# A second layer's loop recast: half images in program order, edge blocks by masked weights, stores on two queues

## The chip, the cores and the metric

The kernel runs on one core of a Trainium2 chip. The metric is the device time of one execution in microseconds (us), the median of the runs. Five engines work side by side: TensorE (PE, with its weight loads as PEld), VectorE (DVE), ScalarE (ACT), GpSimd (POOL) and SyncE (SP). SP and ACT each issue DMAs from their own instruction queue.

## The reference, cut to what matters

Two layers run on a batch of 32 images of 8 channels and 256 x 256 pixels, in f32. Layer 0 (a gated cellular automaton) takes most of the time and is left alone by the change. Layer 1 is a normalised, quantised 3 x 3 convolution with a residual:

```python
x = x + L0(_gn(x), ...)                      # layer 0; its result is called y below
v = _gn(x)                                   # group norm over channel pairs
sx = 127 / max(abs(v)); sw = 127 / max(abs(weight))
qx = clip(round(v * sx), -127, 127)
qw = clip(round(weight * sw), -127, 127)
out = x + (conv3x3(qx, qw) / (sx * sw) + bias)
```

The maximum is taken over all 32 images, so layer 1 can't quantise anything before layer 0 has ended.

## The kernel before, in words

Layer 0 writes its result y to DRAM (`y_s`), image by image, with zero rows above and below, and keeps the mean, the reciprocal deviation and the largest deviation of each image. The second layer (the block `with ExitStack() as two`, from L936) then does one image after the other.

An image is held as 19 blocks (NB) of 128 partitions: 16 rows of 8 channels, the blocks 14 rows apart (STEP), so that a block yields 14 finished rows and its two outer rows are borders; the last block yields 4. One partition of one block is a row of 256 pixels. A 3 x 3 convolution of a block is then three matmuls, one for each horizontal shift, with 128 x 128 weights that join rows and channels.

For image b the loop does this:

- a load (L947) brings all 19 blocks to `yb` (2432 KB, four buffers); the first three are issued by SP, all later ones by ACT, three images ahead;
- DVE subtracts the mean and scales (L978) in three instructions: the first block, the 17 in the middle and the last block, since the first and last use scales (`qs[:, 1]`, `qs[:, 2]`) that are zero for rows outside the image; DVE rounds by adding and subtracting a large constant (L982) and clips into a bf16 tile `qt` whose rows have 258 columns, of which 256 are written (L984);
- PE takes two blocks at a time (10 groups) into one of 4 PSUM buffers, three matmuls each (L991), and ACT brings each group to the f32 tile `ob` with scale and bias (L992); `ob` has two buffers of a whole image;
- DVE adds y to `ob` (L995), and SP stores it in 19 DMAs, one for a block (L998: 18 of 112 KB and one of 32 KB).

The order of instructions on each engine isn't that of the program text: a scheduler places them by its own estimates. In the list that it made, DVE does two additions, then the quantising of two images, and so on in pairs.

Each DMA of SP and ACT signals its landing on one of eight semaphores (called lanes here), which the framework hands out in turn over both queues. A DMA waits on its issuing engine until the DMA that had its lane last, eight places earlier, has landed. Tiles that are used again also wait: `ob` for the stores of two images before.

Of the kernel before, what the change touches and what calls it, by code (L numbers as in the profile page):

```python
# [31 lines left out]
F32 = mybir.dt.float32  # L32
BF16 = mybir.dt.bfloat16
F32R = mybir.dt.float32r
AF = mybir.ActivationFunctionType
ALU = mybir.AluOpType
AX = mybir.AxisListType
DRAM = bass.MemoryType.DRAM
PSUM = bass.MemoryType.PSUM

P = 128
C = 8
# [4 lines left out]
MAX_Q = 127.0  # L47
ROUND = 1.5 * 2.0**23

NB = 19  # L50
STEP = 14
PW = W + 2
# [61 lines left out]
def kernel(  # L114
# [15 lines left out]
    nc = tc.nc  # L130
    B = x.shape[0]
    V, S, G, T = nc.vector, nc.scalar, nc.gpsimd, nc.tensor

    def dram_ap(t, offset, dims):
        return bass.AP(t.tensor, t.offset + offset, dims)
# [5 lines left out]
    masks = cp.tile([P, 4], F32, name="masks")  # L141
# [11 lines left out]
    qw = cp.tile([P, 3, P], BF16, name="qw")  # L153
# [6 lines left out]
    mean_y = cp.tile([P, B], F32, name="mean_y")  # L160
    rstd_y = cp.tile([P, B], F32, name="rstd_y")
# [11 lines left out]
    with tc.tile_pool(name="prep", bufs=1) as pp, tc.tile_pool(name="prep2", bufs=2) as pp2:  # L173
# [24 lines left out]
        for t, n, w in (  # L198
# [3 lines left out]
            k = 64 if w == W else 43  # L202
# [63 lines left out]
    with ExitStack() as one:  # L266
# [4 lines left out]
        pool = lambda name, bufs, **kw: one.enter_context(  # L271
            tc.tile_pool(name=name, bufs=bufs, reuse_waits="tile", **kw)
        )
# [122 lines left out]
        def lattice(g):  # L396
# [81 lines left out]
            if g == 0:  # L478
                units[0], dmas = load(0)
                for d in dmas:  # L480
                    nc.sync.dma_start(*d)
                for ts in tiles:
                    begin(units[0], ts)
            for c in range(C):
                u = g * C + c
                ds = units[u]
                for step in range(STEPS):
                    if step == 7 and u + 1 < NG * C:
                        units[u + 1], dmas = load(u + 1)
                        later.extend(dmas)  # L490
# [375 lines left out]
        def chain(*gens):  # L866
            for gen in gens:
                yield from gen
# [15 lines left out]
        def both(a, t_a, b, t_b):  # L884

            done_a = done_b = 0.0
            while a or b:
                if b is None or a and done_a * t_b <= done_b * t_a:
                    w = next(a, None)
                    if w is None:  # L890
                        a = None
                        continue
                    done_a += w
                else:
                    w = next(b, None)
                    if w is None:
                        b = None
                        continue
                    done_b += w
                yield w  # L900

        def prep(g, groups=((0, 1), (2, 3))):
            return normalise([(b, gs) for gs in groups for b in range(g * GB, g * GB + GB)])

        def images(f, g):
            for b in range(g * GB, g * GB + GB):
                yield from f(b)
# [3 lines left out]
        def after(g, gen):  # L911

            while issued[0] < stored[g]:
                yield 4.0
            yield from gen
# [3 lines left out]
        for g in range(NG):  # L919
            fill, t = images(nca, g), T_NCA  # L920
            if g:
                fill, t = both(fill, t, after(g - 1, images(gate, g - 1)), T_GATE), t + T_GATE
            if g + 1 < NG:
                fill, t = both(fill, t, prep(g + 1), T_PREP), t + T_PREP
            if g == 0:
                fill, t = chain(prep(0, ((1,), (2, 3))), fill), t + 30.0
# [9 lines left out]
    with ExitStack() as two:  # L936


        pool = lambda name, bufs, **kw: two.enter_context(
            tc.tile_pool(name=name, bufs=bufs, reuse_waits="tile", **kw)  # L940
        )
        tp, qp, op, sp, yp = pool("tp", 1), pool("qp", 2), pool("op", 2), pool("sp", 1), pool("yp", 4)
        ps = pool("ps", 4, space=PSUM)

        def load(b):
            y = yp.tile([P, NB, W], F32, name="yb", tag="yb")
            (nc.sync if b < 3 else nc.scalar).dma_start(  # L947
                y, dram_ap(y_s[b], 0, [[W, P], [STEP * C * W, NB], [1, W]])
            )
            return y  # L950

        ys = {b: load(b) for b in range(3)}

        gmax = sp.tile([P, 1], F32, name="gmax")
        V.tensor_reduce(gmax, dev_y, AX.X, ALU.max)
        gall = sp.tile([P, 1], F32, name="gall")
        G.partition_all_reduce(gall, gmax, P, bass.bass_isa.ReduceOp.max)
        sx = sp.tile([P, 1], F32, name="sx")
        V.reciprocal(sx, gall)
        V.tensor_scalar(sx, sx, MAX_Q, None, ALU.mult)  # L960
        inv = sp.tile([P, 1], F32, name="inv")
        V.tensor_tensor(inv, sx, sw, ALU.mult)
        V.reciprocal(inv, inv)
        qs = sp.tile([P, 3, B], F32, name="qs")
        V.tensor_scalar(qs[:, 0, :], rstd_y, sx, None, ALU.mult)
        V.tensor_scalar(qs[:, 1, :], qs[:, 0, :], masks[:, 2:3], None, ALU.mult)
        V.tensor_scalar(qs[:, 2, :], qs[:, 0, :], masks[:, 3:4], None, ALU.mult)
        qt = [qp.tile([P, NB, PW], BF16, name=f"qt{i}", tag=f"qt{i}", bufs=1) for i in range(2)]
        for t in qt:
            V.memset(t[:, :, 0], 0.0)  # L970
            V.memset(t[:, :, PW - 1], 0.0)

        for b in range(B):
            y = ys.pop(b)

            t = tp.tile([P, NB, W], F32, name="tq", tag="tq")
            for k0, k1, i in ((0, 1, 1), (1, NB - 1, 0), (NB - 1, NB, 2)):
                V.tensor_scalar(  # L978
                    t[:, k0:k1, :], y[:, k0:k1, :], mean_y[:, b : b + 1], qs[:, i, b : b + 1],
                    ALU.subtract, ALU.mult,  # L980
                )
            V.tensor_scalar(t, t, ROUND, ROUND, ALU.add, ALU.subtract)  # L982
            q = qt[b % 2]
            V.tensor_scalar(q[:, :, 1 : 1 + W], t, MAX_Q, -MAX_Q, ALU.min, ALU.max)  # L984
            o = op.tile([P, NB, W], F32, name="ob", tag="ob")
            for p in range(10):
                k0, n = 2 * p, (2 if p < 9 else 1)
                pt = ps.tile([P, 512], F32, name="pt2", tag="pt2")
                pt = pt[:, : n * W].rearrange("p (k w) -> p k w", w=W)
                for dx in range(3):  # L990
                    T.matmul(pt, qw[:, dx, :], q[:, k0 : k0 + n, dx : dx + W], start=(dx == 0), stop=(dx == 2))  # L991
                S.activation(o[:, k0 : k0 + n, :], pt, AF.Identity, bias=bv[:, 3:4], scale=inv)  # L992
            if b + 3 < B:
                ys[b + 3] = load(b + 3)
            V.tensor_tensor(o, o, y, ALU.add)  # L995
            for k in range(NB):
                rows = STEP if k < NB - 1 else 4
                nc.sync.dma_start(  # L998
                    dram_ap(out, b * C * H * W + STEP * k * W, [[W, rows], [H * W, C], [1, W]]),
                    o[C : C + rows * C, k, :],  # L1000
                )


# [43 lines left out]
```

## Time and profile before

| what | value |
|---|---|
| median of three runs | 14070.34 us (14065.71 to 14084.15) |
| the profiled execution | 14065.15 us, span 14063.3 us |
| second layer, from its first load's issue | 13284.2 us to the end, some 779 us |
| second layer, from its first scaling (L978) | 13300.35 us to the end, 763 us |
| engine time in 13284 to 14064 us | DVE 523.9, PE 272.6, ACT 219.7, POOL 0.9 us |
| mean DMA rate there | 189 GB/s |

An engine's idle time is put down to what ended it; "q" after an engine's name means its instruction queue, as SP's when it issues a DMA. A chain of waits is followed back from the last instruction: each piece is the work, or the issue or flight of a DMA, that the next one waited for.

### The profile page before, as it was taken

The numbers are of one execution on the slowest core, as the hardware profiler recorded it, in microseconds if no ns is written. First come the engines' busy times: TensorE is split into PE (matmuls) and PEld (weight loads), VectorE is DVE, ScalarE is ACT, GpSimd is POOL, SyncE is SP. The second block draws the span as 40 slices with busy tenths as digits, with TensorE's granted clock in tenths as the row PEclk, the third lists the DMA queues.
The fourth block names the chain that finished last, engine by engine and source line by source line (L and its number), as shares of the span: only waits on it lengthen the run. The fifth ranks groups of instructions, "written<-read, shape, count | busy, mean of one in ns | idle before, by whom it ended". The sixth has DMA issues, their size and how long they took to land. (4 is left out here: it accounts for less than half of the span.)

```text
span 14063.3 us, 229517 instructions
## 1 busy us (share of the span) xinstructions
PE 13110.3 (93%) x81744; PEld 6304.1 (45%) x81744; DVE 8273.9 (59%) x16310; ACT 4036.2 (29%) x6274; POOL 2483.6 (18%) x4270
## 2 busy tenths in 40 slices
PE   5999999999999999999999999999999999999733
PEld 2444444444444444444444444444444444443211
DVE  5555555556556655566556656566556555555566
ACT  2233223222323232332223232332233222221132
POOL 1001111112111111111111211121112111112300
PEclk8999999999999999999999999999999999999966
DMA  6444444444444444444444444444444433333465
GB/s 150 96 103 97 91 108 106 114 94 104 106 110 97 102 105 105 103 103 102 108 100 105 109 99 100 110 107 97 101 108 112 98 81 87 87 84 79 124 188 179
DMA packets 2287208, 1496.74 MB, mean 106 GB/s; under 512 B 1096576, under 2 KB 2257152, under 8 KB 2285952
## 3 DMA queue, kind: packets, MB, share of 16 engines
q1 hardware_dynamic: 2210224, 1409.05, 42.8%
q10 hardware_dynamic: 75856, 73.02, 1.6%
q8 instruction: 664, 10.88, 0.3%
q14 instruction: 464, 3.80, 0.1%
HBM read 866.48 MB, written 478.69 MB: 96 GB/s over the span
## 5 line engine op out<-in xcount | busy, mean ns | idle before, releaser
L511 PE MATMUL pt<-m_a,lw 128*64 128x390 f32 x17280 | 5843.1, 496 | 157.1 <-DMA m_a<-m_a 109.3
L511 PE MATMUL pt<-m_b,lw 128*64 128x384 f32 x17280 | 5808.3, 491 | 18.8 <-DVE m_b L430 17.9
L601 ACT ACTIVATE h<-ph,bp_sb 128x512 f32<-128x512 f32 x4096 | 2585.1, 685 | 5283.9 <-PE ph L591 5209.8
L511 PEld LDWEIGHTS pt<-m_a,lw 128*64 128x64 f32 x17280 | 2298.1, 137 | 1795.2 <-issue 1633.3
L511 PEld LDWEIGHTS pt<-m_b,lw 128*64 128x64 f32 x17280 | 2304.3, 137 | 1649.5 <-issue 1550.6
L519 DVE SCALAR_TENSOR_TENSOR gt<-pt,d_a 128x384 f32<-128x384 f32 x2880 | 1581.5, 549 | 2005.2 <-PE pt L511 2005.0
L519 DVE SCALAR_TENSOR_TENSOR gt<-pt,d_b 128x390 f32<-128x390 f32 x2880 | 1607.0, 558 | 1939.0 <-PE pt L511 1936.4
L591 PE MATMUL ph<-im,wp_hi 48*128 48x512 f32 x12288 | 2621.1, 412 | 89.6 <-DMA im<-xp_s 59.0
L591 PE MATMUL ph<-im,wp_lo 48*128 48x512 f32 x12288 | 2509.9, 395 | 0.0
L528 POOL TENSOR_TENSOR m_b<-m_b,junk 128x12 f32<-128x12 f32 x2688 | 843.6, 314 | 8554.4 <-DVE m_b L524 8156.8
L591 PEld LDWEIGHTS ph<-im,wp_hi 48*128 48x128 f32 x12288 | 1239.8, 186 | 931.5 <-DVE m_b L524 185.8
L524 DVE SCALAR_TENSOR_TENSOR m_b<-gt 128x390 f32<-128x390 f32 x2688 | 1553.5, 578 | 47.0 <-DVE gt L519 0.5
L524 DVE SCALAR_TENSOR_TENSOR m_a<-gt 128x384 f32<-128x384 f32 x2688 | 1541.4, 573 | 18.1
L591 PEld LDWEIGHTS ph<-im,wp_lo 48*128 48x128 f32 x12288 | 1239.6, 186 | 229.9
L608 PE MATMUL acc<-h,wu_z 128*32 128x512 f32 x8320 | 1159.6, 600 | 6.5 <-ACT nca L626 5.5
L799 PE MATMUL pa<-cmb,gw 128*64 128x512 f32 (+1 forms) x3840 | 864.3, 580 | 14.8 <-POOL cmb L723 14.8
L799 PE MATMUL pa<-nb,gw 128*64 128x512 f32 (+1 forms) x3840 | 846.4, 573 | 0.0
L799 PE MATMUL pa<-xnb,gw 128*64 128x512 f32 (+1 forms) x3840 | 841.4, 571 | 0.0
L812 ACT ACTIVATE r<-pa,bv 128x512 f32<-128x512 f32 x320 | 213.2, 666 | 1758.0 <-PE pa L799 1757.9
L991 PE MATMUL pt<-qt,qw 128*128 128x512 bf16 (+1 forms) x960 | 270.9, 453 | 476.2 <-ACT ob L992 424.4
L729 DVE TENSOR_SCALAR xnb<-xb,sc 128x256 f32<-128x256 f32 x608 | 311.9, 528 | 578.0 <-DMA xb<-in_x_dram 569.8
L723 POOL COPY cmb<-cq 128x256 f32<-128x256 f32 x608 | 412.9, 706 | 915.5 <-DMA cq<-cm_s 775.6
(132 smaller groups left out, 7001.6 us busy)
## 6 DMA issues: line engine op xcount, KB each, us to landing
im<-xp_s SPq DMA_DIRECT2D x1152, 193.5 KB
im<-xp_s SPq DMA_DIRECT2D x1216, 96.8 KB
d_a<-xq_s SPq DMA_DIRECT2D x2048, 36.0 KB
nb<-nc_s SPq DMA_DIRECT2D x288, 256.0 KB
cq<-cm_s SPq DMA_DIRECT2D x288, 256.0 KB
yb<-y_s ACTq DMA_DIRECT2D x29, 2432.0 KB
xb<-in_x_dram SPq DMA_DIRECT2D x544, 128.0 KB
xp_s<-hi SPq DMA_DIRECT2D x256, 258.0 KB
```

What stands on the lines that cost most here:

```text
L511: T.matmul(pt[half], lw[:, c, k, half], beside if part == 2 else own, start=part < 2, stop=part > 0,)
L519: V.scalar_tensor_tensor(gt, pt, FLOOR, d[:, ts, :], ALU.max, ALU.add)
L524: V.scalar_tensor_tensor(to, gt, 1.0, gt, ALU.subtract, ALU.mult)
L528: G.tensor_tensor(edge, edge, junk.unsqueeze(1).to_broadcast([P, 6, 2]), ALU.mult)
L591: T.matmul(ph[:, :n].rearrange("p (h w) -> p h w", w=W), w[64 * i : 64 * i + 48, dx, :], rhs[:, :, dx : dx + W], start=(dx == 0 and w is w ...
L601: S.activation(h[:, :n], ph[:, :n], AF.Relu, bias=bp_sb)
L608: T.matmul(acc[32 * g : 32 * g + 32, :cols], wu_z[:, 24 - 8 * i : 56 - 8 * i], h, start=first, stop=last,)
L723: G.tensor_copy(cmb[:, k, 1 : 1 + W].rearrange("p (j q) -> p j q", q=4), cq[:, k, :].rearrange("p (q j) -> p j q", q=4),)
L729: V.tensor_scalar(xnb[:, k, 1 : 1 + W], xb[:, k, :], sc[:, i : i + 1], sc[:, 1:2], ALU.subtract, ALU.mult,)
L799: T.matmul(three[half], gw[:, s * 3 + dx, half], t[:, :n, dx : dx + W], start=(i == 0), stop=(i == 8),)
L812: S.activation(r1[:, : n * W], pa[:, : n * W], AF.Relu, bias=bv[:, 0:1])
L991: T.matmul(pt, qw[:, dx, :], q[:, k0 : k0 + n, dx : dx + W], start=(dx == 0), stop=(dx == 2))
```

## The change

Only the second layer changes. It does the following.

1. The whole block is put under `tc.manual_schedule()`: each engine's instructions keep the order of the program text.
2. An image is worked in two halves, of 10 and 9 blocks. `tq` and `ob` are half images (two and four buffers), `qt` has a tile for each half and parity, and PSUM has 8 buffers.
3. Scaling uses one scale for all blocks. Rounding and the lower clip share an instruction (add, then max), and the upper clip shares one with the subtraction that ends the rounding (min, then subtract). The latter writes `qt` in pieces of 10, 8 and 1 blocks.
4. Rows outside the image are made zero by weights: `qwm` holds two copies of the weights with the rows outside set to zero. The first block of an image and the last have matmuls of their own with them, so an image takes 33 matmuls, of which 9 have 256 columns.
5. The loop is a pipeline by one image. In round b, DVE quantises image b and then adds y to image b-1; SP stores the first 13 blocks of b-1; PE and ACT convolve b; then ACT stores the last 6 blocks of b-1 and loads image b+3 (the buffer that b-1 had).
6. SP issues the first four loads. The zero borders of `qt` are set by POOL instead of DVE.

```diff
+        two.enter_context(tc.manual_schedule())
-        tp, qp, op, sp, yp = pool("tp", 1), pool("qp", 2), pool("op", 2), pool("sp", 1), pool("yp", 4)
-        ps = pool("ps", 4, space=PSUM)
+        tp, qp, op, sp, yp = pool("tp", 2), pool("qp", 1), pool("op", 4), pool("sp", 1), pool("yp", 4)
+        ps = pool("ps", 8, space=PSUM)
...
-            (nc.sync if b < 3 else nc.scalar).dma_start(
+            (nc.sync if b < 4 else nc.scalar).dma_start(
...
+        qwm = sp.tile([P, 2, 3, P], BF16, name="qwm")
+        for i in range(2):
+            V.tensor_scalar(qwm[:, i], qw, masks[:, 2 + i : 3 + i], None, ALU.mult)
...
-            for k0, k1, i in ((0, 1, 1), (1, NB - 1, 0), (NB - 1, NB, 2)):
...
-            V.tensor_scalar(t, t, ROUND, ROUND, ALU.add, ALU.subtract)
-            V.tensor_scalar(q[:, :, 1 : 1 + W], t, MAX_Q, -MAX_Q, ALU.min, ALU.max)
+        HALVES = ((0, 10), (10, NB))
+        def scaled(b, y, h):
...
+            V.tensor_scalar(
+                t, y[:, h0:h1, :], mean_y[:, b : b + 1], qs[:, b : b + 1], ALU.subtract, ALU.mult
+            )
+            V.tensor_scalar(t, t, ROUND, ROUND - MAX_Q, ALU.add, ALU.max)
...
+        def quantised(b, t, h):
+            for k0, k1 in ((0, 10),) if h == 0 else ((0, 8), (8, 9)):
                 V.tensor_scalar(
+                    qt[b % 2][h][:, k0:k1, 1 : 1 + W], t[:, k0:k1, :], ROUND + MAX_Q, ROUND,
+                    ALU.min, ALU.subtract,
                 )
...
+                runs = [(0, n, qw)]
+                if h0 + k0 == 0:
+                    runs = [(0, 1, qwm[:, 0]), (1, n, qw)]
+                elif h0 + k0 == NB - 1:
+                    runs = [(0, 1, qwm[:, 1])]
...
+        last = None
+        for b in range(B + 1):
+            if b < B:
+                y = ys[b]
+                ts = [scaled(b, y, h) for h in range(2)]
+                for h in range(2):
+                    quantised(b, ts[h], h)
+            if last:
+                i, os_ = last
+                yi = ys.pop(i)
+                for h, (h0, h1) in enumerate(HALVES):
+                    o = os_[h][:, : h1 - h0, :]
+                    V.tensor_tensor(o, o, yi[:, h0:h1, :], ALU.add)
+                store(nc.sync, i, os_[0], 0, range(0, 10))
+                store(nc.sync, i, os_[1], 1, range(10, 13))
+            done = last
+            if b < B:
+                last = b, [convolved(b, h) for h in range(2)]
+            if done:
+                i, os_ = done
+                store(nc.scalar, i, os_[1], 1, range(13, NB))
+                if i + 4 < B:
+                    ys[i + 4] = load(i + 4)
```

More of the change, by code (lines that the diff above doesn't have):

```diff
@@ L950, in load @@
             return y
-        ys = {b: load(b) for b in range(3)}
+        ys = {b: load(b) for b in range(4)}
         gmax = sp.tile([P, 1], F32, name="gmax")
@@ L963 @@
         V.reciprocal(inv, inv)
[L964 to L971, printed above, removed]
@@ L973 @@
-        for b in range(B):
-            y = ys.pop(b)
-            t = tp.tile([P, NB, W], F32, name="tq", tag="tq")
-            for k0, k1, i in ((0, 1, 1), (1, NB - 1, 0), (NB - 1, NB, 2)):
+        qs = sp.tile([P, B], F32, name="qs")
+        V.tensor_scalar(qs, rstd_y, sx, None, ALU.mult)
+        qwm = sp.tile([P, 2, 3, P], BF16, name="qwm")
+        for i in range(2):
+            V.tensor_scalar(qwm[:, i], qw, masks[:, 2 + i : 3 + i], None, ALU.mult)
+        qt = [[qp.tile([P, n, PW], BF16, name=f"qt{i}{j}") for j, n in enumerate((10, 9))] for i in range(2)]
@@ new lines @@
+        for t in (*qt[0], *qt[1]):
+            G.memset(t[:, :, 0], 0.0)
+            G.memset(t[:, :, PW - 1], 0.0)
+        HALVES = ((0, 10), (10, NB))
+        def scaled(b, y, h):
+            h0, h1 = HALVES[h]
+            t = tp.tile([P, 10, W], F32, name="tq", tag="tq")[:, : h1 - h0, :]
+            V.tensor_scalar(
+                t, y[:, h0:h1, :], mean_y[:, b : b + 1], qs[:, b : b + 1], ALU.subtract, ALU.mult
+            )
+            V.tensor_scalar(t, t, ROUND, ROUND - MAX_Q, ALU.add, ALU.max)
+            return t
@@ L978 @@
+        def quantised(b, t, h):
+            for k0, k1 in ((0, 10),) if h == 0 else ((0, 8), (8, 9)):
                 V.tensor_scalar(
-                    t[:, k0:k1, :], y[:, k0:k1, :], mean_y[:, b : b + 1], qs[:, i, b : b + 1],
-                    ALU.subtract, ALU.mult,
-                )
[L982 to L985, printed above, removed]
@@ L986, with convolved @@
-            for p in range(10):
-                k0, n = 2 * p, (2 if p < 9 else 1)
+                    qt[b % 2][h][:, k0:k1, 1 : 1 + W], t[:, k0:k1, :], ROUND + MAX_Q, ROUND,
+                    ALU.min, ALU.subtract,
+                )
+        def convolved(b, h):
+            h0, h1 = HALVES[h]
+            o = op.tile([P, 10, W], F32, name="ob", tag="ob")
+            for k0 in range(0, h1 - h0, 2):
+                n = min(2, h1 - h0 - k0)
                 pt = ps.tile([P, 512], F32, name="pt2", tag="pt2")
@@ L989 @@
                 pt = pt[:, : n * W].rearrange("p (k w) -> p k w", w=W)
-                for dx in range(3):
-                    T.matmul(pt, qw[:, dx, :], q[:, k0 : k0 + n, dx : dx + W], start=(dx == 0), stop=(dx == 2))
+                runs = [(0, n, qw)]
[3 more added lines that the diff above has]
+                    runs = [(0, 1, qwm[:, 1])]
+                for i, j, w in runs:
+                    for dx in range(3):
+                        T.matmul(
+                            pt[:, i:j, :], w[:, dx, :],
+                            qt[b % 2][h][:, k0 + i : k0 + j, dx : dx + W],
+                            start=(dx == 0), stop=(dx == 2),
+                        )
@@ L992, with store @@
                 S.activation(o[:, k0 : k0 + n, :], pt, AF.Identity, bias=bv[:, 3:4], scale=inv)
[L993 to L996, printed above, removed]
+            return o
+        def store(queue, b, o, h, ks):
+            for k in ks:
                 rows = STEP if k < NB - 1 else 4
-                nc.sync.dma_start(
+                queue.dma_start(
                     dram_ap(out, b * C * H * W + STEP * k * W, [[W, rows], [H * W, C], [1, W]]),
-                    o[C : C + rows * C, k, :],
+                    o[C : C + rows * C, k - HALVES[h][0], :],
```

## The prediction

> **What bounds the kernel now.** The change touches only the second layer, so I read that stretch first, cut into stretches of 95 to 96 us: the busy time by stretch.
>
> ```profile
> 13615.00:13711.00 96.00, 33.67 (x123) 13.72 (x122) 64.96 (x24) 27.82 (x42) 0.00 (x0) 0.64 0.62 192
> 13711.00:13806.00 95.00, 32.52 (x119) 13.24 (x118) 64.95 (x24) 26.93 (x40) 0.00 (x0) 0.64 0.62 193
> ```
>
> Columns: us, PE, PEld, DVE, ACT, POOL, clock, DMA share, GB/s. The 24 DVE instructions are four images' worth (six each), so an image takes some 23.85 us; DVE works 16.2 to 16.5 of them, PE about 8.3, ACT 6.9, and the DMA engines 62%. No unit is full, so it is a chain of waits. Next view: who waited for whom, first on the engines, then on SP's queue.
>
> ```profile
> ACT ob L992 <- DMA out_dram<-ob: 478.4, 30, 26.3
> PE pt L991 <- ACT ob L992: 424.4, 30, 25.5
> ```
>
> ```profile
> SPq L998 <- DMA yb<-y_s: 124.5, 26, 12.0
> SPq L998 <- DVE ob L995: 49.8, 12, 4.5
> ```
>
> ACT can't bring an image to `ob` before the image two earlier is stored; PE stands behind ACT. The stores are late on SP, and in 26 places a store waited not for data but for a load: it needed that load's lane. The chain of waits, in order of time, shows one such place:
>
> ```profile
> 13605.80 2.12 DMA out_dram<-ob
> 13608.17 0.79 ACT ob L992
> 13609.00 3.88 PE pt L991 x9
> 13612.91 1.64 ACT ob L992 x3
> 13614.54 10.63 DMA yb<-y_s
> 13625.18 0.82 SPq L998
> 13626.11 0.81 SPq L998
> 13626.97 0.82 SPq L998
> ```
>
> A load issued by ACT at 13614.54 lands 10.63 us later, and only then does SP go on storing. SP's bill for an image: 19 stores at 0.895 us from start to start (two in 1.79 us in the chain, 13625.18 to 13626.97), 17.0 us, plus 3.9 us (124.5/32) behind loads, plus some 3 us, most of it waiting for DVE's additions: 23.85. DVE's rows, by form:
>
> ```profile
> L984 DVE TENSOR_SCALAR qt<-tq 128x4864 bf16<-128x4864 f32 x32 | 167.1, 5221 | 123.0 <-PE pt L991 121.4
> L995 DVE TENSOR_TENSOR ob<-ob,yb 128x4864 f32<-128x4864 f32 x32 | 167.1, 5221 | 95.9 <-ACT ob L992 76.9 <-DMA out_dram<-ob 19.0
> L982 DVE TENSOR_SCALAR tq<-tq 128x4864 f32<-128x4864 f32 x32 | 86.2, 2694 | 1.1
> L978 DVE TENSOR_SCALAR tq<-yb,mean_y,qs 128x4352 f32<-128x4352 f32 x32 | 81.3, 2540 | 0.0
> L978 DVE TENSOR_SCALAR tq<-yb,mean_y,qs 128x256 f32<-128x256 f32 x64 | 26.1, 408 | 0.7
> ```
>
> L984 and L982 have one tensor input and equal counts; one takes twice as long.
>
> **What the Trainium skill says.** "VectorE: DVE Perf Modes", What auto-detection actually checks: a one-source operation in SBUF takes the double rate if the outermost counts of source and destination are both even or equal. The trace agrees: L984 writes 19 gapped rows from a tile that can be read as one run and costs 1.07 ns an element; L376 casts 1024 elements into an even number of gapped rows in 0.689 us, 0.67 ns an element with its fixed part. "DMA: Bandwidth & Descriptors", Issuing engines are not separate DMA queues: a second issuing engine saves only issue time, the 16 DMA engines are shared. Here issue time is what SP is short of, and at 62% there is room. Same page, Anatomy of one DMA: a DMA's wait for a semaphore is on the issuing sequencer, so everything behind it stands too; SP's 124.5 us show it, and ACT will now have such waits.
>
> **The change part by part.**
>
> *DVE.* From L982 and L978: a double-rate element is 0.5205 ns, with a fixed part of 0.162 us (constants) or 0.275 us (per-partition scalars); L995 with the 512-element L762 (0.69 us) gives 1.041 ns and 0.157 us at the single rate. Scaling, 2560 and 2304 elements: 1.61+1.47. Rounding with lower clip: 1.50+1.36. Upper clip, 10, 8 and 1 blocks, all even or contiguous: 1.50+1.23+0.30 = 3.03 for 5.22. Additions: 2.82+2.56. Sum 14.35, with 11 gaps of 0.04 us 14.8 us an image (before 16.5). If the clip stays single-rate: 17.2.
>
> *PE.* 24 matmuls of 512 and 9 of 256 columns, at the before's means (0.473 and 0.272) 13.8 busy, though pipelined: 30 matmuls ran in 7.9 to 8.5 us from first to last. Eight PSUM buffers let it run a round ahead. Hidden; it would have to pass 17 us to count.
>
> *SP.* 13 stores for 19: 11.6 us. *ACT.* ten activations (9 x 0.778 + 0.567 = 7.6 us), 6 stores and one load. A store issued by ACT isn't in the trace; the load costs 0.37 on ACT and 0.385 on SP, so I take SP's 0.895. Bounds: SP's shortest and longest issue, 0.65 and 1.12. Six: 5.4 us (3.9 to 6.7). ACT sums to 13.4.
>
> *The new wait.* In the built program's lists, round by round, the lane that ACT's load takes is next given to ACT's own first store of the next round (load on lane 0, next round's first store waits on 0; then 4 and 4). So ACT can't begin its six stores before the previous load has landed, and the next load is issued behind these six. Behind that waiting store stand, on ACT, the load and all activations of the next image, so PE's banks and DVE's additions wait in turn. This is a ring: flight of the load + 6 stores + issue of the load. The ten activations lie in the flight and cost nothing: 7.6 us for some 11. In the semaphore events, loads issued by ACT in 13430 to 13960 land 10.2 to 12.2 us after issue: 10.3 where about 4 stores share the DMA engines, 11.8 where about 8 do. After, some 8 do; I take 11.8. Ring: 11.8 + 5.4 + 0.4 = **17.6 us** a round. DVE (14.8), ACT's work (13.4) and SP (11.6) lie below it. DMA: 4.59 MB (147.11 MB/32) in 17.6 us is 261 GB/s; the busiest 5 us windows reached 357 to 375. SP's stores 9, 11 and 13 get lanes of ACT's stores 4, 5 and 6 of the image before, so SP ends about 2 us after ACT, a round before its `ob` is wanted: hidden.
>
> *Start and end.* POOL's eight memsets (0.131 us for an alike shape) end 1 us after the maximum at 13299.3, long before the first matmul near 13309: nothing. `qwm`: two at up to 0.36 (L224) for the two masked scales (0.47): +0.25, so scaling starts at 13300.6. A fourth load on SP may hold it 8 to 14 us longer, to 13315; its first store is due at 13322. DVE: image 1 quantised at 13319; ACT has it at 13326, stores 0 by 13331.4, issues load 4 at 13331.8. Load 31 is 27 rounds later. From its issue: flight 11.8, six stores 5.4, activations 7.6, six stores 5.4, activations 7.6, then 12.3 (13 stores and 1.6 landing, started 0.9 earlier by the half's addition): 50.1.
>
> Sum: 13331.8 + 27 x 17.6 + 50.1 = 13857. The profiled execution lies 1.85 us above its span (14065.15 and 14063.3), and the median 5.2 above that: 13864, **206 us or 1.5% faster**. Splitting the credit: 6.25 us a round come from SP no longer carrying 19 stores and the load's lane in one queue; the clip's 2.2 us aren't on the ring.
>
> **The rivals.**
>
> A, the floor: the lane wait ends early (short flight, issues of 0.65) and DVE sets the pace, 15.0 us: 13331.8+405+50+7 = 13794. For: both lower bounds together give 14.5. Against: stores now run beside every load. 14%.
>
> B, a longer ring: SP's and ACT's stores both run during the load and stretch it. Upper bounds: a flight of 14.1 (the fourth load at the layer's start) and issues of 1.12 give 21.3: 13964. For: DMA share rises from 62 to some 84%. From 18.8 us (13896) up I count it here. 20%.
>
> C, slower: one mechanism, the load's flight inside the ring. At the start of the layer, with others in the queues, loads took 19.65 and 20.83 us. At 20.8 a round is 26.6 and the time 14107, 0.3% slower. It decides from a flight of about 19.3 (round 25.1). Against: the ring itself allows one load at a time. 3%.
>
> D, the clip doesn't get its double rate: DVE 17.2 us a round, still under 17.6: 13864. It is no gain in time, only in DVE's row; inside the main case.
>
> **How the numbers follow.** Main case, rounds of 16.8 to 18.8: 13842 to 13896, 61%. A 14%, B 20%, C 3%, between (within 0.2%) 2%. The range drops the tips of A and B: 13800 to 13940. What a measurement can tell from no change is about 0.2% (28 us). Faster by more 0.95, within 0.02, slower 0.03.
>
> **What would show it.** Clip rows of about 1.5, 1.2 and 0.3 us; if 2.8, D. ACT idle before L1021 or the next L1015, ended by the load `yb`, some 4 us a round; if it is ended by stores or DVE, the ring is another. Load to load on ACT 17.6 us. SP's waits for `yb` gone. Wrong: a round under 15 or ACT's queue never waiting for a load, or activations that wait for PE.

## The result, and the profile after

| | before | after |
|---|---|---|
| median | 14077.24 us (14065.71 to 14095.38, four runs) | 13869.36 us (13863.82 to 13873.58, four runs) |
| profiled execution | 14065.15 us, span 14063.3 | 13873.58 us, span 13871.8 |
| first load of the second layer issued | 13284.2 | 13305.7 |
| second layer, from there to the end | 779.0 us | 566.1 us |
| load to load, mean from load 4 to load 31 | 23.44 us | 17.55 us |

The ratio is 0.9851 (95% interval 0.9834 to 0.9868), 1.5% faster; 13864 had been forecast. The second layer lost 213 us. Layer 0, untouched, ended some 21 us later in the profiled execution of after than in that of before; in the 14 profiles of this study the second layer's first load lies anywhere from 13263.1 to 13305.7. So below I compare the second layer from its own first load, and say "layer 2" for that time. It is read from one profile of each version. The ratios of the whole runs, each to the kernel before of its own session, give the same differences within 10 us, so a step of 5 us or less isn't clear of noise.

Busy time of after by stretch (columns as before: us, PE, PEld, DVE, ACT, POOL, clock, DMA share, GB/s):

```profile
13500.00:13600.00 100.00, 47.87 (x198) 22.89 (x198) 81.85 (x53) 38.80 (x60) 0.00 (x0) 0.72 0.85 272
```

The DMA share rose from 62% to 85%; still no unit is full. Groups of DVE's instructions by form, from 13340 to 13820 us, those that the change was to alter or that wait:

```profile
L982 DVE TENSOR_SCALAR tq<-yb,mean_y,qs 128x2560 f32<-128x2560 f32 x29 | 46.7, 1612 | 54.0 <-DMA yb<-y_s 54.0
L991 DVE TENSOR_SCALAR qt<-tq 128x2560 bf16<-128x2560 f32 x28 | 41.7, 1490 | 0.0
L991 DVE TENSOR_SCALAR qt<-tq 128x2048 bf16<-128x2048 f32 x28 | 34.2, 1223 | 0.0
L991 DVE TENSOR_SCALAR qt<-tq 128x256 bf16<-128x256 f32 x28 | 8.2, 291 | 0.0
```

The clip (L991) takes 1.49 + 1.22 + 0.29 us: the double rate. The waits in 13340 to 13820 us, on SP's queue:

```profile
SPq L1021 <- DMA out_dram<-ob: 73.8, 53, 2.8
SPq L1021 <- DVE ob L1040: 73.2, 25, 16.8
SPq L1021 <- DMA yb<-y_s: 19.7, 4, 5.9
```

SP's waits for a load are nearly gone (19.7 us in 4, over 480 us; before 124.5 in 26, over 780). The chain of waits from 13500 to 13600 us is one pattern over and over; one round of it:

```profile
13515.57 11.28 DMA yb<-y_s
13526.93 0.83 ACTq L1021
...
13527.86 0.82 ACTq L1021
...
13528.72 0.82 ACTq L1021
...
13529.64 0.82 ACTq L1021
13530.49 0.82 ACTq L1021
...
13531.41 0.68 ACTq L1021
...
13532.13 11.44 DMA yb<-y_s
```

A load takes 11.28 us from the start of its issue to its landing, ACT then issues six stores in 5.2, then the next load. In the order of time ACT's own wait shows as a hole:

```profile
13601.06 0.46 ACTq L948 DMA_DIRECT2D yb<-y_s  x1
...
13601.72 6.58 ACT L1015 ACTIVATE ob<-pt,bv,inv 128x512 f32<-128x512 f32 x10 [10.54 <-DMA out_dram<-ob]
...
13612.67 5.21 ACTq L1021 DMA_DIRECT2D out_dram<-ob  x6
```

The ten activations end at 13608.30, and for 4.4 us ACT does nothing until the load of 13601.06 has landed: by the semaphore events at 13612.60, on the lane that the first of these six stores takes. The profile books ACT's idle time before L1015 to stores (the 10.54 us above; 281.8 us in 27 from 13340 to 13820), which the prediction named as a sign of another ring. It isn't one: the next such stretch, from 13608.30 to the activations at 13618.83, is the hole of 4.4, the six stores' issue of 5.2, the load's issue of 0.7 and 0.2 more, so no landing of a store holds the activations.

The first group above holds something that wasn't forecast. DVE's 54.0 us of waiting are for the load that has just flown: the load issued at 13601.06 lands at 13612.60, and at 13612.70 DVE begins to scale that same image. It is so for every image from image 6 on. The program text asks for a load three images ahead, but ACT is two rounds behind DVE there (its activations from 13601.72 are of image 16), and the load's flight takes the rest of the lead.

### The profile page after: what moved, and what is told of

Read it like the earlier page. It is cut to its first block, busy times and chain, and to the rows that moved or that the text cites. A ratio compares the mean times of both kernels' runs of the same rounds, so it can differ in the third digit from the quotient of the medians.

```text
span 13871.8 us, 229900 instructions
## 1 busy us (share of the span) xinstructions
PE 13115.9 (95%) x81840; PEld 6344.2 (46%) x81840; DVE 8203.1 (59%) x16402; ACT 4023.4 (29%) x6274; POOL 2480.0 (18%) x4278
## 5 line engine op out<-in xcount | busy, mean ns | idle before, releaser
L799 PE MATMUL pa<-cmb,gw 128*64 128x512 f32 (+1 forms) x3840 | 865.6, 580 | 14.7 <-POOL cmb L723 14.7
L608 PEld LDWEIGHTS acc<-h,wu_z 128*32 128x32 f32 x8320 | 253.4, 110 | 612.4 <-issue 542.6
```

The source lines that it names most:

```text
L608: T.matmul(acc[32 * g : 32 * g + 32, :cols], wu_z[:, 24 - 8 * i : 56 - 8 * i], h, start=first, stop=last,)
L799: T.matmul(three[half], gw[:, s * 3 + dx, half], t[:, :n, dx : dx + W], start=(i == 0), stop=(i == 8),)
```

## The experiments

The theory: the chip runs the ring that was forecast, and the gain is the relief of SP's queue. The first rival: the ring on ACT isn't what holds the pace (DMA rate or something else does); the second: the gain comes from the new order of work and not from the second queue.

**e1, the load's lane moved to SP's queue.** The 13th store is issued as two, so that there are 21 DMAs a round and the load's lane next goes to a store of SP.

```diff
+                parts = ((0, 7), (7, 14)) if k in (12,) else ((0, rows),)
+                for r0, r1 in parts:
...
```

> The changed kernel, with one of SP's stores (the thirteenth) issued as two of half its rows: the same bytes, one DMA more in a round, so that in the built program the lane of ACT's load is next given to SP's first store of the following image and no longer to ACT's. Theory (a ring on ACT: load's flight + 6 stores + load's issue sets the round): the ring is cut, and the round falls from 17.5 us (load to load) to what DVE asks for, about 15 us; 27 rounds make 60 to 70 us, so some 13805 us, and the second layer, from its first load, takes 500 to 510 us instead of 566. Rival (the DMA engines, 85% busy, set the round): 17.5 us and 566 us stay, plus or minus 5.

Measured: 13847.21 us (13831.19 to 13855.31), ratio 0.9848 (0.9833 to 0.9863); layer 2 564.6 us for 566.1, round 17.34. A miss for the theory. The rival's 566 came out; its reason, the DMA engines, is tested in e8. The chain of waits shows what took the ring's place:

```profile
13523.77 13.72 DMA yb<-y_s
13537.55 0.83 SPq L1023
...
13540.25 7.05 DMA out_dram<-ob
13547.31 0.83 SPq L1023
...
13552.67 2.34 DMA out_dram<-ob
13555.08 0.82 ACTq L1023
...
13557.89 13.82 DMA yb<-y_s
```

Two rounds in 34.1 us: a load, three stores of SP behind its lane, the flight of a fourth, six more stores, a flight, three of ACT's, the load. The ring wasn't cut but led through the other queue, at the same length.

**e2, the clip in odd counts.** The changed kernel with the clip in 9, 1 and 9 blocks.

```diff
-            for k0, k1 in ((0, 10),) if h == 0 else ((0, 8), (8, 9)):
+            for k0, k1 in ((0, 9), (9, 10)) if h == 0 else ((0, 9),):
```

> The changed kernel with the upper clip cut into odd pieces (9 and 1 blocks, then 9), so that it should run at the single rate: 2.6 us for 9 blocks instead of 1.5 and 1.2. Theory (ring on ACT): DVE goes from 14.8 to about 17.2 us an image, just under the ring's 17.5, so the time changes by less than 15 us. Rival (DVE sets the round): 2.4 us for each of 32 images, plus 77 us.

Measured: 13846.90 us (13843.11 to 13860.2), ratio 0.9852 (0.9835 to 0.9868); layer 2 570.6, 4.5 more, as the theory says. Nine blocks (2304 elements) take 2550 ns where eight take 1223. So the rule on even counts holds here, and the clip's rate is worth almost nothing, though DVE is busy 333 us of the 350 from 13400 to 13750 (after: 281).

**e3, e1 and e2 together.**

> The shifted lanes of the first kernel with the odd clip of the second. Theory: with the ring cut, DVE sets the round, and the 2.4 us now count: round about 17.4 us, 60 to 75 us more than the shifted lanes alone, near the changed kernel's time. Rival (DMA engines set the round): no difference to the shifted lanes alone.

Measured: 13855.92 us (13838.58 to 13868.15), ratio 0.9855 (0.984 to 0.987); layer 2 569.7, 5.0 over e1. A miss: it would have shown DVE at the bound in e1, and e1 had not freed DVE.

**e4, one queue for stores.** The changed kernel with all 19 stores on SP.

```diff
-                store(nc.sync, i, os_[1], 1, range(10, 13))
+                store(nc.sync, i, os_[1], 1, range(10, NB))
...
-                store(nc.scalar, i, os_[1], 1, range(13, NB))
```

> The changed kernel with all 19 stores on SP; ACT issues only the loads. Theory (the gain comes from relieving SP's queue): SP needs 19 x 0.87 = 16.5 us a round, and some 4.7 us more where a store takes the lane of a load in flight: about 21 us a round, some 95 to 100 us slower than the changed kernel, near 13970 us. Rival (the pipeline and the order of the program text gave the gain, the second queue little): under 20 us slower.

Measured: 13909.06 us (13900.96 to 13911.11), ratio 0.9893 (0.9878 to 0.9907); layer 2 627.8, round 19.06. Between the two expectations: of the 213 us, 151 come without any second queue and 62 with it. That goes against the credit in the prediction. SP waits for loads for only 6.5 us in the 390 from 13430 to 13820; it is busy issuing, 267 of the 320 us from 13430 to 13750 by the sum of its stores. The next two runs ask the same from the other side.

**e5, the kernel before with only the clip in 18 and 1 blocks.**

```diff
-            V.tensor_scalar(q[:, :, 1 : 1 + W], t, MAX_Q, -MAX_Q, ALU.min, ALU.max)
+            for k0, k1 in ((0, 18), (18, 19)):
+                V.tensor_scalar(
+                    q[:, k0:k1, 1 : 1 + W], t[:, k0:k1, :], MAX_Q, -MAX_Q, ALU.min, ALU.max
+                )
```

> The kernel before with only the clip cut into 18 blocks and 1 block; nothing else of the change. Theory (the kernel before is bound by SP's queue of stores and loads; the vector engine has some 7 us of idle time in each image): the clip takes 2.8 + 0.3 us for 5.2, and 0 to 15 us come off the whole time. Rival (the additions that SP waits for sit at the end of the vector engine's work, so a shorter clip brings the stores forward): up to 2.1 us an image, 40 to 65 us less.

Measured: 14044.41 us (14032.78 to 14058.57, 20 runs) against 14059.90, ratio 0.9988 (0.9981 to 0.9995); layer 2 760.9, 18 less (15.5 by the medians). At the upper edge of the theory, or just over it.

**e6, the kernel before with only the second queue.**

```diff
-                nc.sync.dma_start(
+                (nc.sync if k < 13 else nc.scalar).dma_start(
```

> The kernel before with only the last six stores of each image moved from SP to ACT; its clip, its tiles and its scheduled order stay. Theory of the prediction (the gain comes from SP's queue being relieved): 18.5 to 19.5 us an image, 130 to 160 us less than before, most of the 213 us that the whole change took off the second layer. Rival from e4 (the order and the half images carry most of it, the second queue about 62 us): 40 to 80 us less than before.

Measured: 14003.91 us (13992.22 to 14010.05), ratio 0.9955 (0.994 to 0.997); layer 2 721.2, 58 less, round 22.12. The rival holds. Its chain of waits says why so little:

```profile
13495.45 12.95 DMA yb<-y_s
13508.42 0.82 SPq L998
...
13514.72 2.50 DMA out_dram<-ob
13517.21 0.77 ACT ob L992
13518.03 6.21 PE pt L991 x18
13524.59 4.81 issue
13529.40 5.22 DVE ob L995
13534.64 0.83 ACTq L998
...
13539.47 0.68 ACTq L998
13540.18 13.42 DMA yb<-y_s
```

In 44.7 us, two images: a load, stores of SP behind its lane, the landing that frees `ob`, an activation, matmuls, DVE's clip, an addition, six stores of ACT, the next load. The clip is what the chain calls issue: in the order of time L984 starts at 13524.26, when the matmuls let it, and takes 5.22 us. The next two images go over a second load (13564.74, 9.44 us) in place of the matmuls and the clip. So PE, ACT and DVE are links of this ring; in the chain of after, with the same split of stores, none of them is.

**e9, the kernel before with nine stores for 19.** One channel of all 18 full blocks a store (252 KB), and the small one; same bytes, all on SP.

```diff
-            for k in range(NB):
...
+            for c in range(C):
+                nc.sync.dma_start(
+                    dram_ap(out, (b * C + c) * H * W, [[W, STEP], [STEP * W, NB - 1], [1, W]]),
+                    o[C + c : C + c + (STEP - 1) * C + 1 : C, : NB - 1, :],
+                )
...
```

> The kernel before, clip and scheduled order kept, with its 19 stores an image on SP made 9 of the same bytes (one channel of all full blocks each). Theory of the prediction (the kernel before is bound by the number of DMAs in SP's queue): SP's stores take some 8 us for 17, the round falls from 23.4 to 16.5 to 18, the second layer from 779 to 560 to 600. Rival, raised by e6 (in the scheduled order an image's load, stores, activations and addition follow each other whatever the queue does): 19 to 22 us a round, second layer 640 to 720.

Measured: 14006.01 us (14005.23 to 14016.01), ratio 0.9962 (0.9947 to 0.9977); layer 2 730.6, 48 less, round 22.19: over the rival's upper end, and far from the theory. SP's issues fell from 15.4 to 10.0 us an image (sums of its stores), the round by only 1.2. So the number of DMAs in SP's queue wasn't what held the kernel before. From the chain of waits:

```profile
13517.34 5.23 DVE ob L995
...
13522.59 13.23 DMA yb<-y_s
13535.83 0.82 SPq L997
...
13539.90 4.29 DMA out_dram<-ob
13544.18 5.21 DVE ob L995
13549.41 10.48 DMA yb<-y_s
```

An addition frees a buffer, so a load starts; SP's next store waits for its lane; the landing of a store, found here ahead of the next addition, lets that begin. Fewer issues shorten one link only; the load of every second round also flies longer, 13 to 14.3 us for some 12 before.

**e10, whole images in the new order.** The changed kernel with one piece of 19 blocks for the two halves.

```diff
-        HALVES = ((0, 10), (10, NB))
+        HALVES = ((0, NB),)
```

> The changed kernel with whole images for halves: one scaling, one rounding, one addition over 19 blocks, clip in 18 and 1 blocks, output tiles of a whole image, two of them for four halves; program order, the two queues and the loads stay. Theory: program order is what counts, halves are worth little, second layer 555 to 590 (the changed kernel: 566). Rival: halves matter, because the first ten stores leave 2.6 us sooner and activations get their tile back sooner: 19 us a round or more, second layer 620 to 660.

Measured: 13894.71 us (13886.83 to 13904.12), ratio 0.9879 (0.9863 to 0.9896); layer 2 609.5, 43 over after, between the two. It isn't a clean undoing: SP's waits for a load came back, since the load's lane fell to SP here (19.7 us in 480 in after):

```profile
SPq L1021 <- DMA yb<-y_s: 93.4, 19, 5.6
```

(13400 to 13750 us.) How much of the 43 is halves and how much is the lane stays open; in e1 the lane's move alone cost nothing.

**e8, half the bytes stored, the same number of DMAs.**

```diff
-                rows = STEP if k < NB - 1 else 4
+                rows = STEP // 2 if k < NB - 1 else 4
```

> The changed kernel with each of its 18 full stores cut to the first 7 of 14 rows: same number of DMAs, some 1.0 MB less of some 4.5 MB an image; it leaves half of the output unwritten. Theory 1 (eight semaphores and the issue of stores): issue is still 0.8 us each, only the load's flight gets about 1 us shorter: round 15.6 to 16.2 for the late 16.8, second layer 530 to 550. Theory 2 (bandwidth): at the same 272 GB/s an image's bytes take 13 us, so the vector engine's 15.0 to 15.3 is the bound and is over 95% busy, second layer 500 to 520.

Measured: 13829.42 us (13812.1 to 13845.67), ratio 0.983 (0.9814 to 0.9847); layer 2 546.0, 20 less; late rounds 16.32 (load 16 to load 31; after 17.04). Theory 1 holds for layer 2, at the upper end of its range; the round is just over it (15.6 to 16.2). Theory 2 is out. By stretch:

```profile
13500.00:13600.00 100.00, 49.45 (x203) 23.44 (x202) 84.39 (x55) 39.56 (x60) 0.00 (x0) 0.74 0.66 215
```

DMA fell from 85% to 66% and 272 to 215 GB/s with hardly any gain. Its chain of waits is the ring of after: load, six stores of ACT at 0.77 to 0.78 us, load.

```profile
13507.65 11.43 DMA yb<-y_s
13519.15 0.77 ACTq L1021
...
13523.40 0.66 ACTq L1021
...
13524.10 12.54 DMA yb<-y_s
```

**e7, nine stores an image in the changed kernel**, five on SP and four on ACT, by channels as in e9, with `ob` a whole image (two buffers):

```diff
-                store(nc.sync, i, os_[0], 0, range(0, 10))
-                store(nc.sync, i, os_[1], 1, range(10, 13))
+                store(nc.sync, i, o, range(5))
...
-                store(nc.scalar, i, os_[1], 1, range(13, NB))
+                store(nc.scalar, i, o, range(5, C + 1))
```

> The changed kernel with 9 stores an image for 19 and the same bytes: a store takes one channel of all 18 full blocks (252 KB), five on SP, three and the small one on ACT. Theory 1 (eight completion semaphores: while a load is in flight only seven other DMAs can be out, and the other twelve are issued outside the flight): with ten DMAs an image the round falls to the vector engine's 15.0 to 15.5 us, the second layer from 566 to 505 to 525 us. Theory 2 (the DMA engines' bandwidth, 85% busy at 272 GB/s): same bytes, round stays at 16.6 to 17.3, second layer 555 to 580. Slower than that would mean that stores with 14 partitions use the DMA engines worse.

Measured: 13792.12 us (13770.53 to 13803.45), ratio 0.9804 (0.9789 to 0.9818), the fastest version here; layer 2 505.1, 61 under after, round 15.26. Same bytes, faster: theory 1's number. But more than the number has changed: the load's lane falls to a store of SP after 26 of ACT's 28 loads (in after it falls to one of ACT's after 24), and `ob` is a whole image. Busy time by stretch:

```profile
13400.00:13500.00 100.00, 59.51 (x221) 26.48 (x220) 92.73 (x62) 44.83 (x69) 0.00 (x0) 0.73 0.94 303
```

DVE is at 93% (89 in the next 100 us) and the DMA engines at 94%: two units near their end. Its chain of waits can't be followed through these rounds in the profile.

**e11, e7 with the clip in odd counts** (the edit of e2).

> The kernel of e7 (nine stores) with the clip in 9, 1 and 9 blocks, odd counts, which cost the vector engine 5.4 us an image for 3.0. Theory (with few DMAs the vector engine is close to the bound, so the clip's rate now counts, which it did not in e2): the vector engine's 16.3 busy us an image at 96 to 97% give 16.8 to 17 a round, second layer 540 to 555 for 505. Rival (bandwidth or the load's flight holds e7 at 15.3): less than 15 us more.

Measured: 13828.94 us (13814.21 to 13839.39), ratio 0.9833 (0.9819 to 0.9848); layer 2 547.7, 43 more than e7: inside the theory's range. DVE is now the bound:

```profile
13500.00:13600.00 100.00, 52.45 (x207) 24.02 (x208) 99.59 (x58) 39.95 (x60) 0.00 (x0) 0.72 0.92 285
```

The same edit cost 4.5 us in e2. What the clip's rate is worth depends on what else holds the pace.

**e12, e7 with all nine stores on SP.**

```diff
-                store(nc.sync, i, o, range(5))
+                store(nc.sync, i, o, range(C + 1))
...
-                store(nc.scalar, i, o, range(5, C + 1))
```

> The kernel of e7 with all nine stores on SP and only loads on ACT. Theory (what a second queue saves is the time in which stores are issued outside the load's flight, and with nine stores there is little of it): 0 to 15 us more than e7, second layer 505 to 520. Rival (a second queue is worth what it was with 19 stores, 62 us): second layer 545 or more.

Measured: 13908.83 us (13901.26 to 13909.86), ratio 0.989 (0.9875 to 0.9905); layer 2 622.2, 117 over e7, round 19.23. A miss for the theory; the rival's bound holds (545 or more), with nearly twice its 62 us. Nine stores on one queue are hardly better than 19 (e4, 627.8). The waits on SP's queue, 13400 to 13750 us, in e12:

```profile
SPq L1022 <- DMA yb<-y_s: 169.3, 18, 10.5
```

and in e7:

```profile
SPq L1022 <- DMA yb<-y_s: 163.4, 21, 10.8
SPq L1022 <- DMA out_dram<-ob: 42.3, 17, 4.4
```

SP stands some 165 us behind loads in both. In e12 all stores stand there, and ACT, then PE and DVE behind it, wait for `ob`; its chain of waits:

```profile
13534.28 15.96 DMA yb<-y_s
13550.30 0.82 SPq L1022
...
13558.46 10.88 DMA out_dram<-ob
...
13569.53 2.95 ACT ob L1014 x5
13572.48 16.24 DMA yb<-y_s
```

A load, SP's stores behind its lane, the flight of one, the activations that it lets begin, and behind them on ACT a load again: two images in 38.2 us. In e7 four stores and the loads go on from ACT. So theory 1's account of e7, by the number of DMAs alone, falls: the few DMAs helped where part of the stores had a queue that the load's lane didn't stop, and not where all of them stood behind it.

## Why the prediction was right, and where its reasons were wrong

Layer 2 in us, from all runs:

| | alone on before (779.0) | taken back from after (566.1) |
|---|---|---|
| clip in even counts | -18 (e5) | +4.5 (e2) |
| stores on two queues | -58 (e6) | +62 (e4) |
| half images | not tried | +43, with the lane's move in it (e10) |

The number came out right partly by luck, as the terms below show.

*What bounds the kernel before: wrong.* The step was "SP's bill for an image", 17.0 + 3.9 + 3 us, read as the limit because it filled the round. By the chains of e6 and e9 it filled it because the waits of a longer ring were booked in it. Taking six stores off SP gave 58 us (e6), taking ten gave 48 (e9). The step that failed is the last sentence of the sum, "6.25 us a round come from SP no longer carrying 19 stores and the load's lane in one queue": the second queue is worth 58 to 62 us of the layer, 1.8 to 1.9 a round. The Trainium skill's warning ("DMA: Bandwidth & Descriptors", Issuing engines are not separate DMA queues: only issue time is saved) was cited and overruled with "issue time is what SP is short of". In after, the six stores' issue is 5.2 us a round, and moving them saved 1.9.

*Where the rest came from.* From e6 to after, same queues, layer 2 fell by 155 us. If at most 43 of that are the halves and 18 the clip (e5), an estimate of 94 us is left for the new order (quantise b, then add b-1, each engine in program order), with what goes with it: the edge blocks by weights, the PSUM buffers, the fourth early load. The clip could have more of it, since it is a link of e6's chain once in two images. The chains fit the order as the cause: matmuls, activation, clip and addition are links of e6's ring and not of after's. But it isn't shown: the new order with nothing else wasn't run, the split stays open, and parts need not add up.

*DVE: right.* The forecast rows 1.50, 1.23, 0.30 came as 1.490, 1.223, 0.291; the sum is 14.33 for 14.35. (The forecast's 11 gaps should have been nine, for nine instructions: 14.7 us for 14.8.) The Trainium skill ("VectorE: DVE Perf Modes", What auto-detection actually checks) has both even or equal outermost counts as the condition; e2's 2550 ns for nine blocks against 1223 for eight agree with it. Rival D is out, and the clip is not on the ring (e2).

*The ring on ACT: right as a chain, too strong as a cause.* It is in the chain line by line, with the 4.4 us hole on ACT that was put at some 4. The flight, from the end of the load's issue, is 10.8 to 11.2 us in most late rounds (12.0 to 12.7 in about every fourth) for 11.8. Six stores take 5.2 for 5.4: from start to start 0.896 us as forecast (13526.93 to 13531.41), but the last, of 32 KB, takes 0.68. The load's issue is 0.46 for 0.4. The mean round, 17.55 for 17.6, is the meeting of two misses and luck: the first five rounds took 19.5, the other 22 17.1. And e1 shows that freeing ACT of this wait alone doesn't shorten the round: the load's lane stops the other queue in its place. By the chains, what holds the pace in after and e1 is that a load keeps a lane for 11 to 13 us and stops whichever queue comes to that lane. It is not bytes (e8) and not DVE (e2). No run gave the load a lane of its own, so this stays argued.

*Start, tail, sum.* Load 4 was due 47.6 us after the first load and came after 43.2; 27 rounds took 473.9 us for 475.2; the tail 49.0 for 50.1. Layer 2 was thus 566.1 for a forecast 572.9, and the later end of layer 0 (+21.4) hid that: span 13871.8 for 13857. The profiled execution was then the slowest of four, so that the median lies 2.4 us below this span, where 7 above was forecast. The median is 5 us from the forecast by these opposite errors. Rival A's floor, 15.0, exists but needs another kernel (e7, 15.26). B's and C's long flights didn't come: none of ACT's loads in after flew for over 13.6 us. Of the signs of being wrong only a trace came: activations waited for PE for 8.2 us in 480.

## What to carry to other kernels

A queue whose work and waits add up to the round isn't thereby the bound: take the waits out, follow the chain around until it closes, and count each engine that is a link. Here moving work to a second queue shortened one link (58 to 62 us of 213); most of the gain came with an order in whose chain the other engines are no links. A load asked for early in the program text helps only as far as the queue that issues it keeps up. Where DMAs share a few completion semaphores in turn, look where the longest transfer's semaphore goes next, and keep what matters off the queue that it stops. Try a saving again after the bound has moved: the clip's rate was worth some 5 us in e2 and 43 in e11.

## What the runs showed of the hardware

- A store of 56 partitions (56 KB) issues in 0.777 us (median, e8), of 112 partitions (112 KB) in 0.81 on SP and 0.82 on ACT (after): half the bytes save 4 to 6% of the issue.
- Stores issued early in a load's flight land 5.5 to 6.2 us after their issue, after its landing 1.6 to 2.3 (after, 13600 to 13623 us). Half the stores' bytes hardly shorten the load's flight: 10.6 to 11.0 us in most late rounds of e8, 10.8 to 11.2 in after. The same bytes in 252 KB stores lengthen it: 15 to 16.6 us in e7's late rounds.
- A 252 KB store of 14 partitions issues in 0.81 us at best, but in up to 2.0 on SP and 2.46 on ACT with others in flight (e7); the 112 KB stores passed 1.02 us only once in after (1.44 us, ACT's first).
